# Scoring some units of a kernel-smoothing attention without the scalar engine: the difference of two clipped copies, accumulated by a second matmul with negated values, in place of an absolute value taken on VectorE

## The chip, the cores and the metric

The kernel runs on one core of a Trainium2 chip. The core has five engines with queues of their own: TensorE (PE; its weight loads are shown apart as PEld), VectorE (DVE), ScalarE (ACT), GpSimd (POOL) and SyncE (SP, which issues most DMAs). Each works off its queue in order and waits on semaphores for the others. The metric is the device time of one execution in microseconds (us). The changed kernel computes the same function.

## The reference, cut to what matters

The reference is a transformer block with two parts: an attention layer without softmax, and a mixture of 64 experts (top 8, capacity 128) with a shared expert. The inputs are 4 sequences of 2048 tokens with 256 features, in float32. The attention has 16 heads of 16 features. Every query and key is projected to one number per head, and with the bandwidth b_h of its head

```python
# out_i = sum_j max(0, 1 - |z_i - z_j|/b_h) * v_j, via prefix sums + searchsorted.
bw = jax.nn.softplus(log_bw) + BW_EPS
...
ctx = ctx / T          # T = 2048
```

where i runs over queries and j over keys. Both parts are followed by a layer norm and a residual sum:

```python
x = x + _layernorm(_L0_attn_ref(_layernorm(x), ...))
x = x + _layernorm(_L0_ffn_ref(_layernorm(x), ...))
```

The kernel does not sort. It forms the weights of all pairs of query and key directly, with q and k already divided by b_h and k negated: the score of a pair is max(0, 1 - |q + k'|) with k' = -k.

## The kernel before, in words

**The score loop.** The time is dominated by a loop of 1024 units, 256 for each of the 4 sequences. A unit is one head h, one tile s of 128 keys, and all 2048 queries. `unit(t)` (L1525) gives the order: two groups g of eight heads, in each two passes p over 4 heads, in each 16 key tiles s, and innermost the four heads j = 0 to 3. So a group is UG = 128 units long and a pass UP = 64; consecutive units have different j.

For a unit, `score(t)` (L1544) fills a tile `hat` of 128 keys by 2048 queries. Usually ACT computes |q + k'| with the key as a per-partition bias (L1558), from a tile `qb` that holds the head's queries copied to all partitions by DMA (`load_q`, L1534). Then DVE forms min(., 1) - 1 in place (L1562); this is minus the score. When a running number `spare`, an estimate of DVE's free time, is 1.3 or more, the unit goes without ACT: DVE adds the key (L1553), clears the sign bit as an integer (L1555), and does L1562 as well. This happens in 65 units; 959 go through ACT.

`product(t)` (L1579) multiplies by the values: the 128 x 32 values of a key tile are the stationary side, 512 queries of `hat` the moving side, and the result is accumulated in PSUM. The four blocks c of 512 queries are not taken from one unit: the product of step t takes block 0 of unit t, block 1 of unit t-1, block 2 of unit t-2 and block 3 of unit t-3. These units have four different j, and j sets which 32 of the 128 PSUM partitions, and so which 32 columns of PE's array, a matmul uses. In float32 a matmul shows as two records in the trace. After the last unit of a group, `evict` (L1564) copies the four accumulators out with a factor of -1/T.

Only after product(t) is the tile of unit t-3 given back. `hat`, `qb` and the evicted results `ct` are taken from one pool of 13 big tiles, first in, first out (`take`, `give`). Near the end of a pass four tiles hold the next heads' queries too.

**The background.** All other work up to the loop's end (the projections of the next sequence, and for finished sequences the layer norm, router, shared expert and experts) is cut into small tasks with an engine, an estimated cost and dependencies, and a planner (`Background`, L26) writes them into the queues between units. `step()` runs once per unit: each engine's `debt` is lowered by its `CAP` and tasks that are ready are emitted as long as the debt stays under it. So CAP is the time per unit that the planner gives an engine for background work: 0.84 us for PE, 0.65 for DVE, 0.30 for ACT; from the third sequence on PE has 0.88. Tasks that L442 names multiply by the weights of a sequence's projection (fours of matmuls of 128 x 32 by 512); those of L573 and L602 belong to the shared expert, L1041 to L1066 to the experts; L1450 and L1481 set up the first sequence's projection. `flush(tasks)` emits given tasks at once, with all that they need. The values of the next sequence are loaded tile by tile on SP as the tiles fall free (L1666); SP's queue is also that of the query loads. What is left after unit 1023 is emitted by `drain()` with other limits.

Of the kernel before, what the change touches and what calls it, by code (L numbers as in the profile page):

```python
# [8 lines left out]
F32 = mybir.dt.float32  # L9
I32 = mybir.dt.int32  # L10
AF = mybir.ActivationFunctionType
ALU = mybir.AluOpType
# [13 lines left out]
class Background:  # L26
# [3 lines left out]
           ("dve", "pe"): 1, ("dve", "sp"): 1, ("pool", "dve"): 2, ("dve", "pool"): 1, ("sp", "dve"): 4,  # L30
           ("sp", "pe"): 4, ("sp", "pool"): 4, ("sp", "act"): 5, ("sp", "sp"): 0, ("pool", "sp"): 1,
           ("act", "sp"): 1, ("pe", "sp"): 1}
    CAP = {"pe": 0.84, "dve": 0.65, "act": 0.30, "pool": 1.5, "sp": 2.0}

    def __init__(self, make):
        self.make = make
# [104 lines left out]
def sandwich_kernel(ctx: ExitStack, tc: tile.TileContext, x_in, wqT, bq, wkT, bk, wvT, bv, wprojT, log_bw,  # L141
# [84 lines left out]
    with ExitStack() as ph:  # L226
# [42 lines left out]
        def give(tag):  # L269
            bg.free["big"].append((tag, bg.t))  # L270
# [11 lines left out]
        vst = [h1[:, i * NP * VW:(i + 1) * NP * VW].rearrange("p (a w) -> p a w", a=NP) for i in range(2)]  # L282
        for t_ in vst:
            nc.gpsimd.memset(t_, 0.0)

        def slot_tile():
            tag, _ = bg.free["slot"][0]
# [1063 lines left out]

        lb = small.tile([P, H], F32, name="lb")
# [23 lines left out]
        nc.sync.dma_start(bvb, bv.rearrange("(a f) -> a f", a=1).to_broadcast([P, F]))  # L1378


        ab = small.tile([P, H], F32, name="ab")
        nc.scalar.activation(ab, lb, AF.Abs)
        ex = small.tile([P, H], F32, name="ex")
        nc.scalar.activation(ex, ab, AF.Exp, scale=-1.0)
        u = small.tile([P, H], F32, name="u")
        nc.vector.tensor_scalar_add(u, ex, 1.0)
        lu = small.tile([P, H], F32, name="lu")
        nc.scalar.activation(lu, u, AF.Ln)
        one = small.tile([P, H], F32, name="one")
        nc.vector.tensor_scalar(one, u, 1.0, None, ALU.is_equal)  # L1390
        nc.vector.tensor_add(lu, lu, one)
        den = small.tile([P, H], F32, name="den")
# [132 lines left out]
        def unit(t):  # L1525
            b, u = divmod(t, NU)
            g, w = divmod(u, UG)
            p, w = divmod(w, UP)
            s, j = divmod(w, 4)
            return b, g, p, s, j, g * GH + 2 * j + p  # L1530
# [9 lines left out]
                                  zq_d[b][m, h:h + 1, :].to_broadcast([P, HK * P]))  # L1540

        spare = [0.0]

        def score(t):  # L1544

            b, g, p, s, j, h = unit(t)
            hat[t] = take(f"hat_{b}_{h}_{s}")
            ht = hat[t][0]
            n = t // UP * 4 + j
            c = s // HK * P + h * HK + s % HK  # L1550
            k = nks[b][:, c:c + 1]
            if spare[0] >= 1.3:
                nc.vector.tensor_scalar(ht, qb[n][0], k, None, ALU.add)  # L1553
                hi = ht.bitcast(I32)
                nc.vector.tensor_scalar(hi, hi, 0x7fffffff, None, ALU.bitwise_and)  # L1555
                spare[0] -= 3.6
            else:
                nc.scalar.activation(ht, qb[n][0], AF.Abs, bias=k)  # L1558
                spare[0] += 1.9 - 1.17
            if s == NT - 1:  # L1560
                give(qb.pop(n)[1])
            nc.vector.tensor_scalar(ht, ht, 1.0, 1.0, ALU.min, ALU.subtract)  # L1562

        def evict(t):  # L1564

            for c in range(4):
                if t - 1 - c >= 0 and (t - 1 - c) % UG == UG - 1:
                    k = (t - 1 - c) // UG
                    b, g = divmod(k, NG)
                    if c == 0:  # L1570
                        ct[b, g] = take(f"ct_{b}_{g}")
                    nc.vector.tensor_scalar(ct[b, g][0][:, c * BK:(c + 1) * BK], pa.pop((k, c)), -1.0 / T, None,
                                            ALU.mult)
                    spare[0] -= 0.63
                    if c == 3 and b < B - 1:
                        nc.sync.dma_start(cx_d[b][g], ct[b, g][0])
                        give(ct.pop((b, g))[1])

        def product(t):  # L1579
            for c in range(4):  # L1580
                tt = t - c
                if not 0 <= tt < B * NU:
                    continue
                b, g, p, s, j, h = unit(tt)
                k, w = divmod(tt, UG)
                if w == 0:
                    pa[k, c] = acc.tile([P, BK], F32, tag=f"pa{c}", name=f"pa_{k}_{c}")
                nc.tensor.matmul(pa[k, c][32 * j:32 * j + 32, :],  # L1588
                                 lhsT=vt[b, s].rearrange("p a w -> p (a w)")[:, h // 2 * VW + p * D:h // 2 * VW + p * D + 32],
                                 rhs=hat[tt][0][:, c * BK:(c + 1) * BK],  # L1590
                                 start=(p == 0 and s == 0), stop=(p == 1 and s == NT - 1))
            if 3 <= t < B * NU + 3:
                give(hat.pop(t - 3)[1])

        nks, last, mst = {0: nk0}, {}, []
        scs0, chain, tabs, stored = [], [], [], [[] for b in range(B)]
# [2 lines left out]
        with tc.manual_schedule():  # L1599
            for n in range(4):  # L1600
                load_q(n)
            for t in range(B * NU + 5):
# [7 lines left out]
                if t == 0:  # L1610
# [26 lines left out]
                    last[0] = [last[0]]  # L1637
                    for i in range(1, B):
                        nks[i], last[i] = prepare(i, after=[last[i - 1]["end"]] if i > 1 else ts[-1:], mdeps=mst)
                if b == 0 and u in (28, 44):  # L1640
                    bg.flush(vts[u // 16 + 1])
                if u == 8 and b > 0:
                    finish(b - 1, after=[last[B - 1]["end"]])
                if u == 0 and b == B - 2:
                    bg.CAP = dict(bg.CAP, pe=0.88, dve=0.75, act=0.4)
                if t == B * NU - 12:
                    env = {}
                    lds = load_last(env)
# [141 lines left out]
```

## Time and profile before

| | |
|---|---|
| median of 3 runs | 2338.87 us (2335.26 to 2339.05) |
| profiled execution | 2339.91 us, span 2338.0 us |
| busy over the span | PE 84%, PEld 29%, DVE 85%, ACT 84%, POOL 21% |
| score loop, first to last min-subtract (L1562) | 66.4 to 2033.7 us |
| score activations on ACT (L1558) | 959, 1992 ns median |
| units without ACT (L1553, L1555) | 65, 1280 and 1227 ns median |
| min-subtract on DVE (L1562) | 1024, 1219 ns median |
| matmuls of the products (L1588) | 4096, two records each, 592 ns median |
| TensorE clock granted | 0.95 of full speed on average |

How to read it: the page covers one execution. Busy time counts instructions that compute. A line of a group gives the source line, engine, operation, the tiles written and read, shapes and count, then busy time and mean duration in ns, then the idle time of the engine just before, with what ended most of it ("<-PE pa" is a wait for a PE instruction on the tile pa). Records of matmuls overlap, because a matmul's end is modelled to include its way through the array; so PE's busy time overstates what PE could not have given to others. Rows of stretches give the stretch, its length, then busy time with the instruction count for PE, PEld, DVE, ACT and POOL in this order, then granted clock, DMA share and GB/s. Rows of the timeline give start, length, engine, line, operation, and the number of records merged.

### The profile page before, as it was taken

What the parts mean: (1) busy time and instruction counts of PE and PEld (TensorE: products, weight loads), DVE (VectorE), ACT (ScalarE), POOL (GpSimd) and SP (SyncE); (2) the same over time, 40 slices, a digit from 0 to 9 for tenths busy, and PEclk for the clock granted to TensorE, in tenths of its full rate; (3) what the DMA queues carried; (4) which work ended last, traced back from release to release, by engine and by line L of the source; (5) the groups of instructions that cost most, each with busy time, mean ns of one, the idle gap of its engine ahead of it and who ended that gap; (6) DMA issues with size and microseconds to landing.
All of it is one profiled execution on the core that took longest, in us unless ns stands there. A gap on an engine that the chain in (4) does not pass through costs nothing. (4 is left out here: it accounts for less than half of the span.)

```text
span 2338.0 us, 32679 instructions
## 1 busy us (share of the span) xinstructions
PE 1952.5 (84%) x12552; PEld 687.2 (29%) x12552; DVE 1996.1 (85%) x3102; ACT 1966.8 (84%) x1269; POOL 490.4 (21%) x339
## 2 busy tenths in 40 slices
PE   7898979888799899677899887878888889987783
PEld 4332323222223222112222222223332223364342
DVE  4799999898999889999989998989999979886335
ACT  2899999898999998999999998989999989742213
POOL 1001010010120000003200003446553234442463
PEclk9999999999999999989999998999999999988897
DMA  4243534427351202142302014465544243355758
GB/s 127 91 133 120 184 103 153 151 88 264 117 162 64 91 19 70 37 147 69 112 19 81 28 54 122 114 186 151 174 121 136 57 134 90 102 177 147 177 124 197
DMA packets 195078, 274.32 MB, mean 117 GB/s; under 512 B 24833, under 2 KB 165505, under 8 KB 194145
## 3 DMA queue, kind: packets, MB, share of 16 engines
q1 hardware_dynamic: 165680, 235.33, 31.2%
q0 software_dynamic: 23824, 31.70, 8.3%
q10 hardware_dynamic: 5408, 5.11, 0.7%
q8 instruction: 101, 1.65, 0.3%
q14 instruction: 65, 0.52, 0.1%
HBM read 189.18 MB, written 82.90 MB: 116 GB/s over the span
## 5 line engine op out<-in xcount | busy, mean ns | idle before, releaser
L1558 ACT ACTIVATE hat<-qb,nk 128x2048 f32<-128x2048 f32 x959 | 1837.3, 1995 | 112.8 <-DMA qb<-zq_d 57.5
L1588 PE MATMUL pa<-hat,v 128*32 128x512 f32 x8192 | 1115.3, 620 | 284.4 <-DVE hat L1562 272.3
L1562 DVE TENSOR_SCALAR hat<-hat 128x2048 f32<-128x2048 f32 x1024 | 1230.3, 1223 | 97.2 <-ACT hat L1558 91.3
L1588 PEld LDWEIGHTS pa<-hat,v 128*32 128x32 f32 x8192 | 186.2, 110 | 900.0 <-DVE hat L1562 652.6
L1066 POOL DMA_INDIRECT y_d<-s,ix x64 | 147.8, 2309 | 286.7 <-DVE s L1064 145.4
L573 PE MATMUL k<-s,sgu 128*128 128x512 f32 x352 | 198.4, 651 | 0.0
L1041 POOL DMA_INDIRECT s<-tab_d,ix x64 | 106.0, 1657 | 327.6 <-DMA qb<-zq_d 259.0
L499 POOL TENSOR_TENSOR rsc<-rsc,mhalf 128x2 f32<-128x2 f32 x24 | 53.4, 2225 | 521.2 <-DVE rsc L498 521.0
L602 PE MATMUL k<-sd,s 128*128 128x256 f32 x384 | 113.7, 428 | 16.9 <-DVE s L589 7.4
L442 PE MATMUL k<-s,s 128*32 128x512 f32 x768 | 102.4, 592 | 0.0
L602 PEld LDWEIGHTS k<-sd,s 128*128 128x128 f32 x384 | 72.2, 205 | 86.4 <-issue 47.8
L573 PEld LDWEIGHTS k<-s,sgu 128*128 128x128 f32 x352 | 54.8, 192 | 136.3 <-issue 121.2
L305 POOL TENSOR_TENSOR rsa<-rsa,mhalf 128x4 f32<-128x4 f32 x16 | 30.8, 1925 | 290.9 <-DVE rsa L304 285.6
L1553 DVE TENSOR_SCALAR hat<-qb,nk 128x2048 f32<-128x2048 f32 x65 | 83.1, 1279 | 0.1
L1555 DVE TENSOR_SCALAR hat<-hat 128x2048 int32<-128x2048 int32 x65 | 79.9, 1229 | 2.2
L350 PE MATMUL k<-h,s 128*128 128x256 f32 x256 | 73.0, 413 | 0.0
L713 DVE MAX8 codes<-scT 128x8 f32<-128x1152 f32 (+2 forms) x48 | 63.4, 1321 | 0.2
L350 PEld LDWEIGHTS k<-h,s 128*128 128x128 f32 x256 | 45.4, 195 | 54.4 <-issue 48.6
L715 DVE MATCH_REPLACE8 scT<-codes,scT 128x1152 f32<-128x1152 f32 (+2 forms) x44 | 57.6, 1310 | 0.0
L607 DVE TENSOR_SCALAR s<-k,gt 128x256 f32<-128x256 f32 x48 | 22.8, 480 | 36.5 <-PE k L602 32.0
L442 PEld LDWEIGHTS k<-s,s 128*32 128x32 f32 x768 | 31.6, 138 | 54.0 <-issue 53.2
L1258 POOL DMA_INDIRECT y_d<-v,ix x28 | 39.9, 1426 | 23.5 <-DMA y_d<-s 7.9
(319 smaller groups left out, 1643.2 us busy)
## 6 DMA issues: line engine op xcount, KB each, us to landing
qb<-zq_d SPq DMA_DIRECT2D x128, 512.0 KB, 5.5
s<-m_d SPq DMA_DIRECT2D x48, 512.0 KB, 4.8
s<-_attn_hidden_states_dram SPq DMA_DIRECT2D x28, 512.0 KB, 5.5
v_d<-h SPq DMA_DIRECT2D x48, 192.0 KB, 2.6
v<-v_d SPq DMA_DIRECT2D x48, 192.0 KB, 2.5
h<-fn_expert_gate_up_w_dram SPq DMA_DIRECT2D x32, 256.0 KB, 3.5
s<-fn_expert_gate_up_w_dram SPq DMA_DIRECT2D x32, 256.0 KB, 2.8
b<-y_d SPq DMA_DIRECT2D x16, 512.0 KB, 9.3
```

The source lines that it names most:

```text
L350: nc.tensor.matmul(env[pk][:, i * F:(i + 1) * F], lhsT=xv[:, k, o:o + P], rhs=wv[:, k, :], start=(k == 0), stop=(k == KF - 1))
L442: nc.tensor.matmul(env[pz][c * CR:(c + 1) * CR, :], lhsT=xv[:, r, :], rhs=env[mp][:, k * 2 * F:(k + 1) * 2 * F], start=(r == 0 and k == 0) ...
L573: nc.tensor.matmul(env[p_], lhsT=sgu[:, k, o:o + P], rhs=featview(env[xT])[:, k, :], start=(k == 0), stop=(k == KF - 1))
L602: nc.tensor.matmul(env[py][:, i * F:(i + 1) * F], lhsT=env[acts[f // 2]][:, o:o + P], rhs=sd[:, f, :], start=(f == 0), stop=(f == NI - 1))
L713: a = bg.add("dve", 1.25, lambda c8=c8: nc.vector.max(out=c8, in_=scT[:, :w]), ev + [a])
L1041: g = bg.add("pool", 1.3, lambda: nc.gpsimd.indirect_dma_start(out=xg(), out_offset=None, in_=tab_d[half][:, :], in_offset=bass.IndirectOf ...
L1066: s = bg.add("pool", 1.9, lambda: nc.gpsimd.indirect_dma_start(out=y_d[half][:, :], out_offset=bass.IndirectOffsetOnAxis(ap=iv(), axis=0), ...
L1553: nc.vector.tensor_scalar(ht, qb[n][0], k, None, ALU.add)
L1555: nc.vector.tensor_scalar(hi, hi, 0x7fffffff, None, ALU.bitwise_and)
L1558: nc.scalar.activation(ht, qb[n][0], AF.Abs, bias=k)
L1562: nc.vector.tensor_scalar(ht, ht, 1.0, 1.0, ALU.min, ALU.subtract)
L1588: nc.tensor.matmul(pa[k, c][32 * j:32 * j + 32, :], lhsT=vt[b, s].rearrange("p a w -> p (a w)")[:, h // 2 * VW + p * D:h // 2 * VW + p * D ...
```

## The change

Let n = -k' be the key. Two clipped copies of the queries are formed: low = q held between n-1 and n, and hat = q held between n and n+1. For q above n, low is n and hat - low is min(q - n, 1); for q below n, hat is n and hat - low is min(n - q, 1). So hat - low = min(|q + k'|, 1), and minus the score is hat - low - 1. A clipped unit therefore makes two tiles, `low` and `hat`, with one DVE instruction each, reading two per-partition operands (columns of n-1, n, n+1), and accumulates both: `hat` with the values and `low` with the negated values. The missing -1 times the sum of the values of all clipped units is taken off when a group is evicted.

In detail:

- In `score`, a unit with `spare` of 1.3 or more takes the clipped form if it lies between units 4 and 115 of its group and if the pool has at least 3 to 5 free big tiles; otherwise it takes the old form. It takes a second big tile, forms the three columns (a DVE operation on 128x3), negates the 128x32 values (DVE), adds the values to a running sum per head (POOL), and clips twice (DVE). `spare` is lowered by 2.7 (3.6 for the old form), and PE's debt is raised by 1.1.
- In `product`, each of the four blocks of a clipped unit gets a second matmul ahead of its own, with the same destination. The low tile is given back together with the hat tile.
- At unit 120 of each group `sums` multiplies the sums with a column of ones (four small matmuls) and DVE copies the result to `csum`; this is flushed in place. POOL clears the sums at the start of a group.
- `evict` subtracts `csum` (a per-partition operand) before the factor -1/T.
- PE's CAP goes from 0.84 to 0.86, and from the third sequence on from 0.88 to 0.92.
- A new small tile `pro` holds the sums, the columns and two buffers of negated values, and before the loop the temporaries of the bandwidth, which had tiles of their own.

In the order of instructions that results, 62 units are clipped, 17 take the old form and 945 go through ACT.

```diff
-    CAP = {"pe": 0.84, "dve": 0.65, "act": 0.30, "pool": 1.5, "sp": 2.0}
+    CAP = {"pe": .86, "dve": 0.65, "act": 0.30, "pool": 1.5, "sp": 2.0}
...
+        pro = small.tile([P, 12 * D + 8], F32, name="pro")
+        near = const.tile([P, 3], F32, name="near")
+        csum = const.tile([P, 1], F32, name="csum")
+        for i in range(3):
+            nc.gpsimd.memset(near[:, i:i + 1], i - 1.0)
...
+        def value(t):
+
+            b, g, p, s, j, h = unit(t)
+            o = h // 2 * VW + p * D
+            return vt[b, s].rearrange("p a w -> p (a w)")[:, o:o + 2 * D]
+
+        def sums():
+
+            env = {}
+
+            def mm():
+                for j in range(4):
+                    nc.tensor.matmul(env["cs"][2 * D * j:2 * D * j + 2 * D, :1], lhsT=pro[:, 2 * D * j:2 * D * j + 2 * D],
+                                     rhs=near[:, 2:3], start=True, stop=True)
+            q, bg.q = bg.q, []
+            a = bg.add("pe", 0.4, mm, get={"cs": "bank"}, env=env)
+            a = bg.add("dve", 0.15, lambda: nc.vector.tensor_copy(csum, env["cs"][:, :1]), [a], put=["cs"], env=env)
+            bg.q += q
+            bg.flush([a])
...
-            if spare[0] >= 1.3:
-                nc.vector.tensor_scalar(ht, qb[n][0], k, None, ALU.add)
-                hi = ht.bitcast(I32)
-                nc.vector.tensor_scalar(hi, hi, 0x7fffffff, None, ALU.bitwise_and)
-                spare[0] -= 3.6
+            u = t % NU
+            if u % UG == 0:
+                nc.gpsimd.memset(pro[:, :8 * D], 0.0)
+            room = 3 + (s >= 9) + (u % UG >= UG - 24)
+            if spare[0] >= 1.3 and 4 <= u % UG < UG - 12 and len(bg.free["big"]) >= room and (True):
+
+                low[t] = take(f"low_{b}_{h}_{s}")
+                i = len(clipped) % 2
+                kk = pro[:, 12 * D + 4 * i:12 * D + 4 * i + 3]
+                neg[t] = pro[:, (8 + 2 * i) * D:(10 + 2 * i) * D]
+                tot = pro[:, 2 * D * j:2 * D * j + 2 * D]
+                nc.vector.tensor_scalar(kk, near, k, None, ALU.subtract)
+                nc.vector.tensor_scalar(neg[t], value(t), -1.0, None, ALU.mult)
+                nc.gpsimd.tensor_tensor(out=tot, in0=tot, in1=value(t), op=ALU.add)
+                nc.vector.tensor_scalar(low[t][0], qb[n][0], kk[:, 0:1], kk[:, 1:2], ALU.max, ALU.min)
+                nc.vector.tensor_scalar(ht, qb[n][0], kk[:, 1:2], kk[:, 2:3], ALU.max, ALU.min)
+                clipped.add(t)
+                spare[0] -= 2.7
+                bg.debt["pe"] += 1.1
             else:
-                nc.scalar.activation(ht, qb[n][0], AF.Abs, bias=k)
-                spare[0] += 1.9 - 1.17
+                if spare[0] >= 1.3:
...
+                    spare[0] -= 3.6
+                else:
+                    nc.scalar.activation(ht, qb[n][0], AF.Abs, bias=k)
+                    spare[0] += 1.9 - 1.17
+                nc.vector.tensor_scalar(ht, ht, 1.0, 1.0, ALU.min, ALU.subtract)
...
-                    nc.vector.tensor_scalar(ct[b, g][0][:, c * BK:(c + 1) * BK], pa.pop((k, c)), -1.0 / T, None,
-                                            ALU.mult)
+                    nc.vector.tensor_scalar(ct[b, g][0][:, c * BK:(c + 1) * BK], pa.pop((k, c)), csum, -1.0 / T,
+                                            ALU.subtract, ALU.mult)
...
+                if tt in low:
+                    nc.tensor.matmul(pa[k, c][32 * j:32 * j + 32, :], lhsT=neg[tt], rhs=low[tt][0][:, c * BK:(c + 1) * BK],
+                                     start=False, stop=False)
...
+                if u % UG == UG - 8:
+                    sums()
...
-                    bg.CAP = dict(bg.CAP, pe=0.88, dve=0.75, act=0.4)
+                    bg.CAP = dict(bg.CAP, pe=.92, dve=0.75, act=0.4)
```

More of the change, by code (lines that the diff above doesn't have):

```diff
@@ L1350, in norm_x0 @@
             xt0.append(done)
-        lb = small.tile([P, H], F32, name="lb")
+        lb, ab, ex, u, lu, one, den = (pro[:, i * H:(i + 1) * H] for i in range(7))
         nc.sync.dma_start(lb, log_bw.rearrange("(a h) -> a h", a=1).to_broadcast([P, H]))
@@ L1378, in sandwich_kernel @@
         nc.sync.dma_start(bvb, bv.rearrange("(a f) -> a f", a=1).to_broadcast([P, F]))
-        ab = small.tile([P, H], F32, name="ab")
         nc.scalar.activation(ab, lb, AF.Abs)
-        ex = small.tile([P, H], F32, name="ex")
         nc.scalar.activation(ex, ab, AF.Exp, scale=-1.0)
-        u = small.tile([P, H], F32, name="u")
         nc.vector.tensor_scalar_add(u, ex, 1.0)
-        lu = small.tile([P, H], F32, name="lu")
         nc.scalar.activation(lu, u, AF.Ln)
-        one = small.tile([P, H], F32, name="one")
         nc.vector.tensor_scalar(one, u, 1.0, None, ALU.is_equal)
         nc.vector.tensor_add(lu, lu, one)
-        den = small.tile([P, H], F32, name="den")
         nc.vector.tensor_scalar_sub(den, u, 1.0)
@@ L1542, in sandwich_kernel @@
         spare = [0.0]
+        low, neg, clipped = {}, {}, set()
+        def value(t):
[13 more added lines that the diff above has]
+            bg.flush([a])
         def score(t):
@@ L1551, in score @@
             k = nks[b][:, c:c + 1]
-            if spare[0] >= 1.3:
-                nc.vector.tensor_scalar(ht, qb[n][0], k, None, ALU.add)
-                hi = ht.bitcast(I32)
-                nc.vector.tensor_scalar(hi, hi, 0x7fffffff, None, ALU.bitwise_and)
-                spare[0] -= 3.6
-            else:
-                nc.scalar.activation(ht, qb[n][0], AF.Abs, bias=k)
-                spare[0] += 1.9 - 1.17
+            u = t % NU
[16 more added lines that the diff above has]
+                bg.debt["pe"] += 1.1
+            else:
+                if spare[0] >= 1.3:
+                    nc.vector.tensor_scalar(ht, qb[n][0], k, None, ALU.add)
+                    hi = ht.bitcast(I32)
+                    nc.vector.tensor_scalar(hi, hi, 0x7fffffff, None, ALU.bitwise_and)
+                    spare[0] -= 3.6
[3 more added lines that the diff above has]
+                nc.vector.tensor_scalar(ht, ht, 1.0, 1.0, ALU.min, ALU.subtract)
             if s == NT - 1:
                 give(qb.pop(n)[1])
-            nc.vector.tensor_scalar(ht, ht, 1.0, 1.0, ALU.min, ALU.subtract)
         def evict(t):
@@ L1587, in product @@
                     pa[k, c] = acc.tile([P, BK], F32, tag=f"pa{c}", name=f"pa_{k}_{c}")
[L1588 to L1591, printed above, removed]
+                first_, last_ = p == 0 and s == 0, p == 1 and s == NT - 1
+                if tt in low:
+                    nc.tensor.matmul(pa[k, c][32 * j:32 * j + 32, :], lhsT=neg[tt], rhs=low[tt][0][:, c * BK:(c + 1) * BK],
+                                     start=False, stop=False)
+                nc.tensor.matmul(pa[k, c][32 * j:32 * j + 32, :], lhsT=value(tt), rhs=hat[tt][0][:, c * BK:(c + 1) * BK],
+                                 start=first_, stop=last_)
             if 3 <= t < B * NU + 3:
                 give(hat.pop(t - 3)[1])
+                if t - 3 in low:
+                    give(low.pop(t - 3)[1])
         nks, last, mst = {0: nk0}, {}, []
```

## The prediction

> **What bounds the kernel now.** I read first the busy shares, then the score loop alone (64 to 2034 us, units 0 to 1023), then its groups by line and shape, then who waited, then short timelines. The profiled execution took 2339.9 us, a span of 2338.0 and 1.9 around it; the median of the runs is 2338.9, so 1.0 is taken off at the end.
>
> ```profile
> 64.00:2034.00 1970.00, 1684.59 (x11323) 525.11 (x11327) 1798.16 (x2415) 1871.45 (x1082) 356.49 (x195) 0.97 0.36 110
> ```
>
> This row (length, then busy PE, PEld, DVE, ACT, POOL, then clock and DMA) covers 84% of the time. ACT is busy 95% of it, DVE 91%, PE 86%. Three engines are near full, so the bound changes from stretch to stretch. The groups give the prices:
>
> ```profile
> L1558 ACT ACTIVATE hat<-qb,nk 128x2048 f32<-128x2048 f32 x959 | 1837.3, 1995 | 112.8 <-DMA qb<-zq_d 57.5 <-PE pa L1588 49.6 <-DMA cx_d<-ct 3.1
> L1588 PE MATMUL pa<-hat,v 128*32 128x512 f32 x8192 | 1115.3, 620 | 284.4 <-DVE hat L1562 272.3
> ```
>
> ```profile
> L1562 DVE TENSOR_SCALAR hat<-hat 128x2048 f32<-128x2048 f32 x1024 | 1230.3, 1223 | 97.2 <-ACT hat L1558 91.3
> L1553 DVE TENSOR_SCALAR hat<-qb,nk 128x2048 f32<-128x2048 f32 x65 | 83.1, 1279 | 0.1
> L1555 DVE TENSOR_SCALAR hat<-hat 128x2048 int32<-128x2048 int32 x65 | 79.9, 1229 | 2.2
> L309 DVE TENSOR_SCALAR s<-s,mva,rsa 128x256 f32<-128x256 f32 x64 | 23.4, 412 | 2.3 <-POOL rsa L305 2.3
> L607 DVE TENSOR_SCALAR s<-k,gt 128x256 f32<-128x256 f32 x48 | 22.8, 480 | 36.5 <-PE k L602 32.0
> ```
>
> An ACT unit costs ACT 1837.3/959 = 1.916 us and DVE 1.20; one of the 65 units without ACT costs DVE 1.28 + 1.23 + 1.20 = 3.71. PE's price needs the timeline, where the count is of half-matmuls (each matmul shows as two records):
>
> ```profile
> 71.31 1.05 PE L1588 MATMUL pa<-hat,v 128*32 128x512 f32 x4
> 74.45 1.06 PE L1588 MATMUL pa<-hat,v 128*32 128x512 f32 x6 [1.03 <-DVE hat L1562]
> 76.58 1.06 PE L1588 MATMUL pa<-hat,v 128*32 128x512 f32 x8
> ...
> 391.57 1.92 PE L1588 MATMUL pa<-hat,v 128*32 128x512 f32 x16
> ...
> 393.58 3.90 ACT L1558 ACTIVATE hat<-qb,nk 128x2048 f32<-128x2048 f32 x2 [0.27 <-PE pa L1588]
> ```
>
> Two, three or four matmuls of one product take the same 1.05 us: they go to different 32-column groups of the array and run side by side. Two products back to back take 1.92, so a further turn of the same column groups costs 1.92 - 1.06 = 0.86. The last line shows ACT itself held by PE, through a tile that PE had not released. That happens where background matmuls are dense. Units 16-47, 96-127, 176-191 and 272-287, same columns as above:
>
> ```profile
> 101.40:156.20 54.80, 54.80 (x524) 23.04 (x524) 52.22 (x52) 52.52 (x29) 0.00 (x0) 1.00 0.25 87
> 244.90:299.30 54.40, 54.40 (x504) 18.54 (x504) 50.94 (x47) 49.06 (x27) 0.00 (x0) 1.00 0.59 181
> 389.30:418.30 29.00, 29.00 (x266) 9.84 (x268) 24.93 (x26) 25.33 (x14) 0.00 (x0) 1.00 0.59 190
> 574.20:598.30 24.10, 24.10 (x228) 8.01 (x224) 23.34 (x21) 23.43 (x13) 0.00 (x0) 1.00 0.58 175
> ```
>
> In these 162 us PE is never idle, while ACT has 12.0 us left and DVE 10.9.
>
> **The change, part by part.** Counts are from the changed kernel's instruction order.
>
> ACT: 945 score activations in place of 959. Only 14 go, because 62 clipped units and 17 of the old form replace 65: at most 14 x 1.916 = -26.8 us. Where they go matters more; see below.
>
> DVE: the old form loses 65 - 17 = 48 pairs, 48 x 2.51 = -120.5; the min-subtract loses 62, 62 x 1.20 = -74.5. Each clipped unit adds two clips with two per-partition operands and two small operations. A clip appears nowhere. L309 has two such operands and two operations on 256 elements: 412 ns. L607, whose source is PSUM, has one operand and takes 480. So L309 passes elements faster than L607; if L1562's 2048 elements in 1223 ns and L309 share a rate, and two operands add twice the 56 ns by which L1553 exceeds L1562, a clip is 1223 + 112 = 1335 ns. The other end is L607's rate: twice the streaming, about 2.4 us. I take 1.34, as L309 is the nearest row in form. The small ones I put at 0.2 each (128x4 operations take 168 to 216 ns). A clipped unit is 2 x 1.34 + 0.4 = 3.08, and 62 are +191. Evictions gain a pointer operand, 32 x 0.06 = +2. DVE sum: -2 us, nothing.
>
> PE: 248 further matmuls of 128x32 by 512. Each goes to the same column group as the one behind it in its product, since both accumulate into the same 32 partitions. It can't run beside it. So each costs 0.86, a clipped unit 3.44 over its four products, 213 us in all; the floor is the average of a packed matmul, 1115.3/4096 = 0.27, or 67 us. I take 0.86. The planner is told 1.1 per clipped unit, so it moves only 68 us of background aside.
>
> By the Trainium skill (TensorE: Matmul & The Clock Gate, Part 3, What overlaps and what doesn't) matmuls start and end strictly in program order, which would put the other three matmuls of a product behind the pair as well. By that rule nothing of the 213 us could be hidden inside a product; by the trace's packed average it would be 67. No row of before shows two matmuls of one product on one column group.
>
> Where that falls: the background matmuls that fill PE now lie at units 10-57 (L1450, L1481), 104-139, 188-231 and 280-317 (L442), against 10-50, 96-128, 176-208 and 256-288 before. In these zones are 7, 3, 9 and 4 clipped units. What PE needs there, against the time that the same units took before (starts of their L1562):
>
> - 188-231: 44 products x 0.86 + 32 background fours x 0.86 + 9 x 3.44 = 37.8 + 27.5 + 31.0 = 96 us; before 85. +11.
> - 280-317: 32.7 + 27.5 + 13.8 = 74; before 69. +5.
> - 104-139: 31.0 + 27.5 + 10.3 = 69; before 65. +4.
> - 10-57: 41.3 + 36 (before's rate there, 1.71 a unit less 0.86, over 41 units, and 1 for the rest) + 24.1 = 101; before 85. +16.
>
> And in units 400-447 (the shared expert's matmuls) PE had 3.4 us idle of 91; five clipped units add 17.2, of which the planner moves 5.5 aside: +8.
>
> Sum +44. The tiles let PE fall behind: a tile comes back to ACT 4.8 units after its release (counted in the order), some 9 us, of which one unit's way through ACT, DVE and PE needs 1.9 + 1.2 + 1.1, so about 5 are margin. A stretch may end that much late and make it up in the emptier units behind; I take 3 for each of the five: +29. The other 34 clipped units lie where PE has 10 to 40% idle; I cost them at nothing, the cover being that idle time. Without cover each costs up to 3.44 - 1.1 = 2.34, 80 us.
>
> The ACT saving, zone by zone: inside the four zones the units without ACT go from 16 to 29, so 13 of the 14 lie where PE sets the pace, and outside it is one: -2 us.
>
> New waits: eight times a loop a group's value sum is flushed in place. DVE's copy of it stands behind four small matmuls and the product before them, about 1.06 + 0.66 (four small transposes at L1047 show 0.66), then 0.2: 15 us in which DVE's queue, and behind it the next min-subtracts, stand. DVE's 172 idle us cover it at one end, 15 at the other; I take +5. POOL gets 62 adds of 128x32 (its 128x2 to 128x256 rows are 0.2 to 2.2 us); nobody waits but that flush, 12 units later, and 17 of the 48 value loads on SP, which now also wait for POOL, with query loads queued behind them: 0.
>
> The end: two more of the experts' turns and four more shared matmuls lie after the loop, in 304 us that hold 68 turns; the matmuls are four of 1.1 us: between 0 and 13, +2 as PE is 75% busy there.
>
> Sum: 29 - 2 (ACT) + 5 + 2 - 2 (DVE) = **+32**: 2339.9 + 32 - 1.0 = **2371 us**.
>
> **The rivals.**
>
> *PE hides it (faster).* In zone 188-231 the clipped units cost nothing as long as one takes PE under (85 - 65.3)/9 = 2.2 us, 0.55 per matmul. For it: column groups are served side by side, so those without the pair can run ahead, and by total PE has 285 idle us for 213. Against it: the background is of full width and needs all groups. Then ACT's -26.8 stands, with the +7 of flushes and end: 2319.
>
> *Tiles run short (no change).* One of 13 big tiles is held for four units more. From a tile's release to its next score the order gives 5.2 units on average before, 4.8 after; four units: 95 cases to 266, three or less: 68 to 97. In the trace ACT's wait before a score grows from 0.07 us at five units to 0.37 at four and 0.51 at three. Weighted with where in a phase they lie, that is +24, which cancels ACT's gain even if PE hides its part: 2337.
>
> *Clips at half the rate (slower still).* 124 x 1.07 = +133 us on DVE, against 172 idle; in the zones it adds to PE's loss: about +75, 2414. L309 speaks against it.
>
> *POOL holds SP.* At the change to the last batch POOL is in its gathers, where one wait for DVE was 14.4 us; a value load behind it holds the query loads: +14 on the main case, 2385.
>
> **How the numbers follow.** PE's column cost 0.48, PE hides it 0.33, no change 0.10, half-rate clips 0.05, POOL 0.04. The likeliest gives 2371, on its own 2354 (the five stretches use their whole 5 us of margin, flushes and end cost nothing) to 2394 (ten clipped units more uncovered). The range, 2314 to 2405, takes in the faster case and leaves out the half-rate clips and the tails. 0.2% (4.7 us) is about what a measurement tells from no change: faster 0.33, same 0.10, slower 0.57.
>
> **What would show it.** Score activations 945; clips near 1.34 us (2.4 would be the half rate). A product with a clipped unit about 1.9 us long, not 1.06. PE busy in the loop near 1850 us and fully busy over units 188-231, and those 44 units some 8 us longer; ACT's waits for PE well over 49.6. If a product of ten records takes under 1.6 us, or the zones run no longer than before, the main step is wrong.

## The result, and the profile after

The changed kernel takes **2470.09 us** (median; 2466.93 to 2476.59), against 2338.96 us (2335.26 to 2342.61) for the kernel before: a ratio of 1.0564, 95% interval 1.0536 to 1.0593. It is slower by 131 us, where the forecast said 32 slower, and lies above the range. The profiled execution has a span of 2466.2 us, 128.2 more than before.

Of these 128.2 us, 119 lie in the score loop (first score to last, 1970.6 us before and 2089.7 after), 11 after it (303.2 and 314.6), and 2 are gained ahead of it. Busy times of the page after:

```profile
PE 2131.2 (86%) x13112; PEld 754.8 (31%) x13112; DVE 1988.5 (81%) x3200; ACT 1947.4 (79%) x1253; POOL 523.4 (21%) x412
```

PE is busy 179 us more (1952.5 before), which is only 2% more of the longer span (84% before), and DVE and ACT fell from 85 and 84% to 81 and 79: by these shares no engine became the bound. The same row for the loop alone (length, then busy PE, PEld, DVE, ACT, POOL, clock, DMA):

```profile
63.90:2150.40 2086.50, 1857.13 (x11861) 591.29 (x11861) 1788.21 (x2508) 1851.20 (x1064) 381.51 (x258) 0.98 0.34 103
```

PE's 1857 us are near the 1850 that the prediction named, and 172.5 more than before: 0.70 for each of the 248 matmuls, where its price of 0.86 gives 213. So PE got no more work than was foreseen; what the work does to the time was not foreseen. The groups of after (busy us, mean ns, idle time before them and who ended it):

```profile
L1600 ACT ACTIVATE hat<-qb,nk 128x2048 f32<-128x2048 f32 x945 | 1818.1, 1995 | 242.5 <-PE pa L1634 144.9 <-DMA qb<-zq_d 59.1 <-PE pa L1632 13.5
L1634 PE MATMUL pa<-hat,v 128*32 128x512 f32 x8192 | 1307.5, 614 | 223.5 <-DVE hat L1602 213.4 <-DVE ct L1614 3.8 <-DVE hat L1589 2.5
L1602 DVE TENSOR_SCALAR hat<-hat 128x2048 f32<-128x2048 f32 x962 | 1161.0, 1223 | 151.3 <-ACT hat L1600 148.0
L1588 DVE TENSOR_SCALAR low<-qb,pro 128x2048 f32<-128x2048 f32 x62 | 84.3, 1360 | 9.2 <-PE pa L1634 7.3 <-PE pa L1632 1.3
L1589 DVE TENSOR_SCALAR hat<-qb,pro 128x2048 f32<-128x2048 f32 x62 | 83.2, 1341 | 0.0
```

The clips cost what was expected. But ACT now stands 144.9 us behind PE's products (49.6 before), and DVE stands 148.0 behind ACT (91.3 before). The products' own group grew by 192 us in busy time (1115.3 before) although it has no instruction more: a matmul that has to wait for the one on its column group spreads its product out. Here is one such product (start, length, records of half-matmuls), with the background matmul behind it:

```profile
435.64 0.62 PE L1634 MATMUL pa<-hat,v 128*32 128x512 f32 x1
435.65 0.62 PE L1632 MATMUL pa<-low,pro 128*32 128x512 f32 x1
435.66 1.03 PE L1634 MATMUL pa<-hat,v 128*32 128x512 f32 x3
436.10 0.59 PE L1632 MATMUL pa<-low,pro 128*32 128x512 f32 x1
436.12 1.44 PE L1634 MATMUL pa<-hat,v 128*32 128x512 f32 x4
437.48 1.13 PE L357 MATMUL k<-h,s 128*128 128x256 f32 x4
```

From the product's start to the background matmul's it is 1.84 us; a product without a pair takes 1.07 (median of those standing alone) and one with a pair 1.92 (median of all 248). The rule of the Trainium skill that the prediction weighed (TensorE: Matmul & The Clock Gate, Part 3, What overlaps and what doesn't: matmuls start and end in program order) fits this in size. The order itself is not shown by this row: the two records of `low` start 0.45 us apart, with three of `hat` between them. So that the background matmul waits behind the pair is seen; whether the product's other matmuls do stays open.

Where in the loop the time went, by the starts of the min-subtracts (the second clip for a clipped unit):

| units | before, us | after, us | difference | predicted |
|---|---|---|---|---|
| 10-57 | 85.3 | 99.6 | +14.4 | +16 |
| 104-139 | 65.2 | 74.0 | +8.8 | +4 |
| 188-231 | 85.2 | 93.9 | +8.7 | +11 |
| 280-317 | 68.9 | 77.7 | +8.8 | +5 |
| 400-447 | 91.3 | 101.7 | +10.4 | +8 |
| the five, with lag made up | | | +51 | +44 - 15 |
| 448-511 | 117.2 | 129.5 | +12.3 | 0 |
| 704-767 | 121.0 | 136.9 | +15.9 | 0 |
| 960-1022 | 122.3 | 138.7 | +16.4 | 0 |
| all else | | | +23 | 0 |

The five stretches that were called full lost 51 us, and the units behind each of them took longer too: 58-103 by 6.7 us, 140-187 by 3.7, 232-279 by 5.0, 318-399 by 0.3. In 188-231 PE is busy all the time, as foreseen:

```profile
439.80:533.70 93.90, 93.90 (x681) 34.01 (x679) 69.95 (x75) 67.74 (x36) 5.30 (x7) 1.00 0.37 118
```

The rest of the loop, costed at about nothing, lost 68. The stretch 704-767 before and then after shows why this is not seen in busy shares:

```profile
1408.60:1529.60 121.00, 96.15 (x656) 30.36 (x648) 105.30 (x116) 108.65 (x67) 52.31 (x25) 0.93 0.46 123
```

```profile
1492.20:1629.10 136.90, 111.87 (x703) 33.79 (x699) 105.48 (x136) 109.08 (x66) 49.01 (x27) 0.96 0.38 104
```

PE was 79% busy there. It got 15.7 us more to do, had 24.9 us idle, and the stretch became longer by 15.9: the added work came on top, and the idle time stayed (25.0 us after).

### The profile page after: what moved, and what is told of

Same layout as the page of the kernel before. It is cut to its first block, busy times and chain, and to the rows that moved or that the text cites. A ratio compares the mean times of both kernels' runs of the same rounds, so it can differ in the third digit from the quotient of the medians.

```text
span 2466.2 us, 33990 instructions
## 1 busy us (share of the span) xinstructions
PE 2131.2 (86%) x13112; PEld 754.8 (31%) x13112; DVE 1988.5 (81%) x3200; ACT 1947.4 (79%) x1253; POOL 523.4 (21%) x412
## 5 line engine op out<-in xcount | busy, mean ns | idle before, releaser
L1600 ACT ACTIVATE hat<-qb,nk 128x2048 f32<-128x2048 f32 x945 | 1818.1, 1995 | 242.5 <-PE pa L1634 144.9
L1634 PE MATMUL pa<-hat,v 128*32 128x512 f32 x8192 | 1307.5, 614 | 223.5 <-DVE hat L1602 213.4
L1602 DVE TENSOR_SCALAR hat<-hat 128x2048 f32<-128x2048 f32 x962 | 1161.0, 1223 | 151.3 <-ACT hat L1600 148.0
L1634 PEld LDWEIGHTS pa<-hat,v 128*32 128x32 f32 x8192 | 240.0, 109 | 892.0 <-DVE hat L1602 534.1
L1632 PE MATMUL pa<-low,pro 128*32 128x512 f32 x496 | 258.4, 603 | 4.3 <-DVE low L1588 4.1
L449 PE MATMUL k<-s,s 128*32 128x512 f32 x768 | 164.1, 598 | 0.0
L609 PE MATMUL k<-sd,s 128*128 128x256 f32 x352 | 101.7, 418 | 9.4 <-DVE s L614 9.4
L1588 DVE TENSOR_SCALAR low<-qb,pro 128x2048 f32<-128x2048 f32 x62 | 84.3, 1360 | 9.2 <-PE pa L1634 7.3
L1589 DVE TENSOR_SCALAR hat<-qb,pro 128x2048 f32<-128x2048 f32 x62 | 83.2, 1341 | 0.0
L449 PEld LDWEIGHTS k<-s,s 128*32 128x32 f32 x768 | 50.0, 140 | 50.8 <-issue 49.0
L1632 PEld LDWEIGHTS pa<-low,pro 128*32 128x32 f32 x496 | 42.8, 109 | 71.3 <-issue 49.0
```

Of the source, the lines that this page charges most:

```text
L449: nc.tensor.matmul(env[pz][c * CR:(c + 1) * CR, :], lhsT=xv[:, r, :], rhs=env[mp][:, k * 2 * F:(k + 1) * 2 * F], start=(r == 0 and k == 0) ...
L609: nc.tensor.matmul(env[py][:, i * F:(i + 1) * F], lhsT=env[acts[f // 2]][:, o:o + P], rhs=sd[:, f, :], start=(f == 0), stop=(f == NI - 1))
L1588: nc.vector.tensor_scalar(low[t][0], qb[n][0], kk[:, 0:1], kk[:, 1:2], ALU.max, ALU.min)
L1589: nc.vector.tensor_scalar(ht, qb[n][0], kk[:, 1:2], kk[:, 2:3], ALU.max, ALU.min)
L1632: nc.tensor.matmul(pa[k, c][32 * j:32 * j + 32, :], lhsT=neg[tt], rhs=low[tt][0][:, c * BK:(c + 1) * BK], start=False, stop=False)
L1634: nc.tensor.matmul(pa[k, c][32 * j:32 * j + 32, :], lhsT=value(tt), rhs=hat[tt][0][:, c * BK:(c + 1) * BK], start=first_, stop=last_)
```

## The experiments

Four theories stood after the result. *Column theory*: the second matmul on a column group is what costs, and PE's idle time takes none of it. *Tile theory*: the second tile held for four units. *Placement theory*: the planner's new limits and the units' places. And the *flush* of the sums. In the table, loop and end (after the last score) are from the profiled executions; where a kernel leaves out a part of the computation, the work after the loop still has the changed kernel's number of matmuls and of indirect transfers unless it is said otherwise. Each ratio is to the kernel before in the same round of runs. Its median was 2333.8 to 2339.0 us over the rounds, so a difference between medians of two rounds is good to some 5 us.

| run | ratio to before, 95% interval | median us | loop us | end us | PE busy us |
|---|---|---|---|---|---|
| before | 1 | 2338.96 | 1970.6 | 303.2 | 1952.5 |
| after | 1.0564 (1.0536-1.0593) | 2470.09 | 2089.7 | 314.6 | 2131.2 |
| a1_one_column | 1.0128 (1.0108-1.0148) | 2366.35 | 1993.3 | 308.3 | 1972.0 |
| a2_no_tile | 1.0519 (1.0499-1.0540) | 2458.24 | 2082.3 | 306.9 | 2115.4 |
| a6_no_tile_one_column | 1.0023 (1.0007-1.0038) | 2339.10 | 1961.9 | 314.8 | 1960.0 |
| a4_old_only | 1.0116 (1.0096-1.0136) | 2362.91 | 1977.7 | 319.6 | 1950.5 |
| e1_pairs | 1.0550 (1.0519-1.0582) | 2463.98 | 2099.9 | 303.2 | 2119.4 |
| e2_packed | 1.0131 (1.0089-1.0173) | 2363.39 | 2001.7 | 307.0 | 1998.6 |
| e3_tile_held | 1.0078 (1.0051-1.0105) | 2354.86 | 1990.0 | 300.7 | 1956.5 |
| a3_no_flush | 1.2834 (1.2799-1.2870) | 2999.53 | 2070.3 | 859.9 | 2323.5 |
| e4_outside | 1.0343 (1.0317-1.0369) | 2413.70 | 2045.3 | 301.5 | 2056.1 |
| e6_spread | 1.0307 (1.0273-1.0340) | 2405.32 | 2046.1 | 300.6 | 2108.3 |
| b1_limits | 1.0105 (1.0085-1.0125) | 2359.84 | 1975.4 | 318.6 | 1950.1 |
| g1_two_units | 1.0354 (1.0334-1.0374) | 2417.73 | 2040.4 | 312.8 | 2055.9 |
| c1_limits_back | 1.0507 (1.0476-1.0537) | 2450.74 | 2084.8 | 300.7 | 2125.2 |
| c3_two_units_limits_back | 1.0544 (1.0515-1.0573) | 2461.38 | 2068.5 | 327.3 | 2061.9 |
| c2_lower | 1.0014 (0.9996-1.0032) | 2340.55 | 1972.3 | 303.8 | 1955.0 |

### One column in place of 512 (a1_one_column)

```diff
-nc.tensor.matmul(pa[k, c][32 * j:32 * j + 32, :], lhsT=neg[tt], rhs=low[tt][0][:, c * BK:(c + 1) * BK],
+nc.tensor.matmul(pa[k, c][32 * j:32 * j + 32, :1], lhsT=neg[tt], rhs=low[tt][0][:, c * BK:c * BK + 1],
```

> The changed kernel with its 248 extra products cut from 512 columns to one: low*(-v) is left out but for one column in 512. The clips, the second tile, the order and the planner's numbers stay. Column theory (the 0.85 us that a product with a pair takes beyond one without is time that nothing hides, 213 us of PE in all): PE loses about 200 us of busy time, a product with a pair falls from 1.92 to about 1.1 us, and most of the +131 goes: 2340 to 2375 us. Tile theory (62 units hold two of the 13 big tiles, so the writers run out of tiles): the tiles are held as long as before, so 2440 to 2470. Placement theory (the planner's limits and the units taken off ScalarE in the wrong stretches): 2430 to 2470.

Measured 2366.35 us: 104 of the 131 are gone with nothing changed but the width of 248 matmuls. Of the loop 96.4 us go, for 159 us of PE. A product whose pair is one column wide, again with the background matmul behind it:

```profile
413.76 0.62 PE L1634 MATMUL pa<-hat,v 128*32 128x512 f32 x2
413.78 0.19 PE L1632 MATMUL pa<-low,pro 128*32 128x1 f32 x1
413.79 0.62 PE L1634 MATMUL pa<-hat,v 128*32 128x512 f32 x1
413.83 0.17 PE L1632 MATMUL pa<-low,pro 128*32 128x1 f32 x1
413.86 1.02 PE L1634 MATMUL pa<-hat,v 128*32 128x512 f32 x5
414.82 1.13 PE L357 MATMUL k<-h,s 128*128 128x256 f32 x4
```

It is 1.06 us to the next matmul in place of 1.84 (at the median 1.05, against 1.00 behind a product without a second matmul). So the columns streamed a second time through a column group are the cost, not the instruction.

### No second tile, alone and with one column (a2_no_tile, a6_no_tile_one_column)

```diff
-                low[t] = take(f"low_{b}_{h}_{s}")
+                low[t] = hat[t]
...
-                    give(low.pop(t - 3)[1])
+                    low.pop(t - 3)
```

> The changed kernel without a second tile: the first clip is written to the unit's own tile, the second clip overwrites it, and both matmuls of the pair read that tile, so low is lost. Instructions and their counts stay. Column theory: as the changed kernel, 2440 to 2470, with products of a pair at 1.9 us. Tile theory: most of the +131 goes, 2350 to 2390. Both in parts: in between; then the shares of this run and of the run with one column are to be added and set against the run with both.

> Both edits at once: no second tile, and the extra products one column wide (low's part of the computation is left out). If columns and tiles are all that the change costs: 2335 to 2360 us. If the placement of the units, the planner's limits or the sums cost as well, it stays above 2380. If the effects of the two edits add up, the saving is the sum of those of the two single edits; if either alone frees the same wait, it is that of the larger one.

Alone, the missing tile saves 12 us (7.4 of the loop). Together with the narrow matmuls it saves 27 more than these alone do (31.4 of the loop), and the kernel is back at 2339 us. So the tile is a second, smaller cost, and it shows fully only where PE doesn't already set the pace. With both gone the loop is 8.7 us shorter than before, flush and limits included, where the 14 activations fewer are 26.8 us of ACT's busy time. It is 24 us shorter in the five stretches, where all of these 14 lay (20 units without ACT before, 34 after), and 16 longer elsewhere, where 18 us of the flush fall.

### The old form alone, and the limits alone (a4_old_only, b1_limits)

The first is the changed kernel with no unit clipped, the second the kernel before with two numbers changed:

```diff
-            if spare[0] >= 1.3 and 4 <= u % UG < UG - 12 and len(bg.free["big"]) >= room and (True):
+            if spare[0] >= 1.3 and 4 <= u % UG < UG - 12 and len(bg.free["big"]) >= room and (False):
```

```diff
-    CAP = {"pe": 0.84, "dve": 0.65, "act": 0.30, "pool": 1.5, "sp": 2.0}
+    CAP = {"pe": .86, "dve": 0.65, "act": 0.30, "pool": 1.5, "sp": 2.0}
...
-                    bg.CAP = dict(bg.CAP, pe=0.88, dve=0.75, act=0.4)
+                    bg.CAP = dict(bg.CAP, pe=.92, dve=0.75, act=0.4)
```

> The changed kernel with no clipped unit at all: units not done by ScalarE take the old form (add, then mask), csum stays zero and its flush is left out; the planner's limits .86 and .92, the new order of small tiles and the longer eviction stay. Placement theory in so far as it is the planner's limits: slower than before by 20 us or more. Column and tile theories: within 10 us of before, 2330 to 2349.

> The kernel before with the changed kernel's planner limits for PE (.86 for .84 and .92 for .88) and nothing else. If the limits alone make the end after the score loop longer (it took 320 us in the changed kernel without clipped units, against 303): 2350 to 2365, with an end of 315 to 320 us. If not: within 5 us of before, and the 16 us come from elsewhere in the changed code.

The old form alone is 27 us slower than before, which neither column nor tile theory allows; the limits alone cost 26 (15.4 in the end, 4.8 in the loop, by the profiles; the profiled execution of before lies 6 us above the median of that round). So the limits explain it, and the other small edits (small tiles, the pointer operand of the eviction) nothing that can be seen. The stretch after the loop, before and then with the new limits:

```profile
2034.90:2338.00 303.10, 218.79 (x855) 131.85 (x852) 168.69 (x586) 81.54 (x164) 124.65 (x110) 0.85 0.66 160
```

```profile
2039.50:2358.10 318.60, 221.20 (x863) 132.76 (x863) 169.95 (x588) 81.61 (x165) 129.25 (x112) 0.84 0.63 153
```

PE has 2.4 us more to do there and POOL 4.6, and the end is 15.5 longer. So the amount of work left over doesn't account for it. Its order may; that was not traced.

### Pairs, packed matmuls and held tiles in the kernel before (e1_pairs, e2_packed, e3_tile_held)

```diff
+                if tt in old:
+                    nc.tensor.matmul(pa[k, c][32 * j:32 * j + 32, :], lhsT=zw, rhs=hat[tt][0][:, c * BK:(c + 1) * BK],
+                                     start=False, stop=False)
```

```diff
+            for c in range(4):
+                if t - 3 in old:
+                    k, j = (t - c) // UG, (t - c) % 4
+                    nc.tensor.matmul(pa[k, c][32 * j:32 * j + 32, :], lhsT=zw, rhs=hat[t - c][0][:, c * BK:(c + 1) * BK],
+                                     start=False, stop=False)
```

```diff
+                if len(bg.free["big"]) >= 3 + (s >= 9) + (t % UG >= UG - 24):
+                    idle[t] = bg.free["big"].pop(0)[0]
...
+                    if t - 3 in idle:
+                        give(idle.pop(t - 3))
```

`old` holds the units of the old form, `zw` zero weights. The first stands ahead of a block's own matmul, the second after the four of a product.

> The kernel before with 224 further matmuls with zero weights, one in each of the four products of the 56 units in the old form that lie where the changed kernel allows a pair; each goes to the same column group as its own matmul. The result is unchanged, no tile, clip or unit is added. Column theory: products with such a pair take 1.9 us in place of 1.07, PE gains 224 x 0.86 = 193 us of busy time, and the kernel is slower by 70 to 120 us, 2410 to 2460. Tile theory and placement theory: within 20 us of before, as PE's slack takes it.

> The kernel before with the same number of matmuls with zero weights as in the run of pairs, but the four of a unit's step lie in four different column groups, as a further product of four. Column theory: 56 further turns of about 0.86 to 1.07 us, 48 to 60 us of PE, and the kernel is slower by 10 to 40 us; a quarter to a third of what the pairs cost. If the number of matmuls or of their columns counts, and not the column group: the same as the pairs.

> The kernel before with an unused big tile taken out of the pool at each unit in the old form, by the changed kernel's rule for room, and given back with the unit's own tile four units later. No instruction is added. Tile theory: slower by 40 us or more, with ScalarE waiting longer on PE at the units after. Column theory and placement theory: within 10 us of before.

224 pairs bring the kernel before to 2464 us, nearly the changed kernel's time, with none of its clips, tiles, sums or limits; the end is untouched. As many matmuls on four different column groups cost 25 us in place of 126. So it is the further turn that is paid. A further turn costs PE 0.75 us as a pair (166.9/224) and 0.82 as a packed four (46.1/56), close to the 0.86 of the prediction. The held tiles cost 17 us, between the two theories' values; the pairs cost a little more than the column theory's range.

### Pairs where PE has idle time, and pairs spread out (e4_outside, e6_spread)

```diff
-                if 4 <= t % UG < UG - 12:
+                if 4 <= t % UG < UG - 12 and not (10 <= t <= 57 or 104 <= t <= 139 or 188 <= t <= 231 or 280 <= t <= 317 or 400 <= t <= 447):
                     old.add(t)
```

```diff
-                if tt in old:
+                if tt % 4 == 0 and 4 <= tt % UG < UG - 12 and c == tt // 4 % 4:
```

> The kernel before with the pairs of zero-weight matmuls at the 38 old-form units alone that lie outside the five stretches which the prediction counted as full (10-57, 104-139, 188-231, 280-317, 400-447): 152 further matmuls. Cost at nothing there, as the prediction had it (PE has 10 to 40% idle at them): within 10 us of before. If PE's idle time can't take them: the 72 us that the run with all 56 units lost outside the five stretches, so 2400 to 2420, 1.9 us for each unit.

> The kernel before with 224 zero-weight matmuls again, but one in every fourth unit (one of its four products) in place of four in each of 56 units: the same work for PE in small pieces. If the cost is PE's time on average: as the run of pairs, 2440 to 2480. If it is the burst, four products running in which PE falls 3.4 us behind while the 13 tiles hold only some units of work: much less, 2350 to 2400.

The first tests the very step that cost nothing in the prediction. Its 38 units lie outside the five stretches, and the loop is 74.7 us longer (the median 80): 2.0 us for each unit, 0.72 us for each us that PE got to do. PE's idle time hid a quarter. (11 of the 74.7 us fall inside the five stretches, where no pair stands; outside them it is 64, 1.7 for each unit.) Why it hides so little is seen at unit 749. Before (start, length, engine, instruction, idle before it):

```profile
1503.52 1.23 DVE L1562 TENSOR_SCALAR hat<-hat 128x2048 f32<-128x2048 f32 x1
1505.51 0.48 DVE L1064 TENSOR_SCALAR s<-k,s 128x256 f32<-128x256 f32 x1 [0.76 <-PE k L1061]
1505.91 1.22 DVE L1562 TENSOR_SCALAR hat<-hat 128x2048 f32<-128x2048 f32 x1
```

and with the pair of that unit:

```profile
1547.78 1.23 DVE L1567 TENSOR_SCALAR hat<-hat 128x2048 f32<-128x2048 f32 x1
1552.32 0.48 DVE L1064 TENSOR_SCALAR s<-k,s 128x256 f32<-128x256 f32 x1 [3.32 <-PE k L1061]
1552.72 1.22 DVE L1567 TENSOR_SCALAR hat<-hat 128x2048 f32<-128x2048 f32 x1
```

The middle instruction belongs to an expert of the background and takes a result of PE (k). PE's matmul for it comes 2.5 us later here, behind the four widened products; and DVE takes its queue in order, so the next min-subtract stands behind that. It isn't a tile that is late here, and no stock of tiles helps. The waits of DVE for such results over the whole execution, before and with these pairs (total us, times, longest):

```profile
DVE s L607 <- PE k L602: 32.0, 22, 3.6
...
DVE s L1054 <- PE k L1047: 12.0, 16, 2.2
DVE s L1064 <- PE k L1061: 11.0, 13, 2.7
```

```profile
DVE s L607 <- PE k L602: 39.1, 25, 3.8
DVE s L1064 <- PE k L1061: 30.5, 26, 4.6
DVE s L1054 <- PE k L1047: 21.4, 19, 2.8
```

Summed over the loop, DVE's waits for PE ahead of such instructions are 69 us before, 123 here, 130 after (16.6 of them for csum), and 86 in the changed kernel with one column (14.7 for csum). ACT's waits for tiles rose too: 49.6 us before, 144.9 after, and here

```profile
ACT hat L1563 <- PE pa L1596: 99.2, 84, 5.7
```

That is 50 us more, as much as DVE's 54. No run took one of the two away and left the other, so the share of each stays open.

The same matmuls one at a time, in every fourth unit, give PE nearly as much (155.8 us) and cost the loop 75.5 us in place of 129. The time, 2405 us, lies between the two expectations. A single further turn (0.70 us) is hidden by half, four in a row by a quarter. The runs differ in place as well: of the 224 turns 50 lie in the five stretches here, 72 in the run of pairs. Outside the stretches a spread turn costs 0.25 us (43.7/174), one of four in a row 0.42 (63.7/152, from the run of 38 units). That the spread ones lie mostly at units done by ACT, and the pairs at units of the old form, was not tested apart.

### Without the flush (a3_no_flush)

```diff
-                if u % UG == UG - 8:
-                    sums()
```

> The changed kernel without the sums of the values and their flush, eight times (csum stays zero, so the correction by the sum of the values is left out). If the flush costs what its idle time before DVE says (16.6 us over eight): 2450 to 2462. If it is taken up by the waits beside it: 2465 to 2475. If it empties the pipeline each time (more than 5 us each): below 2430.

The total misled: 2999.53 us. Without the correction the context is another, and with it what the router decides: after the loop there are 182 indirect transfers in place of 53, in 859.9 us in place of 314.6 (in the loop 117 and 118). Only the loop can be compared: 2070.3 us, 19.4 shorter than after, and 17.8 of this lie around the flushes, from unit 116 of each group to unit 11 of the next. So the eight flushes cost about 2.4 us each, near the 16.6 us for which DVE stands before them:

```profile
DVE csum L1562 <- PE k L1558: 16.6, 8, 3.8
```

### Two units in a row, and the limits back (g1_two_units, c1_limits_back, c3_two_units_limits_back, c2_lower)

```diff
-            if spare[0] >= 1.3 and 4 <= u % UG < UG - 12 and len(bg.free["big"]) >= room and (True):
+            second = t - 1 in clipped and t - 2 not in clipped
+            if (second or spare[0] >= 1.3 and 4 <= u % UG < UG - 12 and len(bg.free["big"]) >= room + 1) and len(bg.free["big"]) >= 2:
...
         def product(t):
             for c in range(4):
                 tt = t - c
+                if tt in low:
+                    k, j = tt // UG, tt % 4
+                    nc.tensor.matmul(pa[k, c][32 * j:32 * j + 32, :], lhsT=neg[tt], rhs=low[tt][0][:, c * BK:(c + 1) * BK],
+                                     start=False, stop=False)
+            for c in range(4):
+                tt = t - c
...
-                if tt in low:
-                    nc.tensor.matmul(pa[k, c][32 * j:32 * j + 32, :], lhsT=neg[tt], rhs=low[tt][0][:, c * BK:(c + 1) * BK],
-                                     start=False, stop=False)
```

These are the edits of the first run. The second sets the two limits of the changed kernel back to .84 and .88, the third does both, and the last sets those of the kernel before to .82 and .86.

> The changed kernel with the clipped units taken two in a row (28 times two, 56 in all, for 62 single ones), and the extra matmuls of a product set ahead of its four ordinary ones, so that two units need five further turns for eight extra matmuls (140 in all for 248). The result is unchanged. Column theory with shared turns: PE loses about 80 us of busy time, and the kernel gains 30 to 50 us on the changed one, 2420 to 2440. If each extra matmul costs its own time: 2455 or more. Tile theory: slower than the changed kernel, as four tiles are held for two units at once.

> The changed kernel with the planner's limits for PE of before (.84 and .88), all else as changed. If the 26 us that the limits cost in the kernel before are a part of the changed kernel's loss: 2440 to 2450, with an end near 303 us after the loop. If the clipped units use up what the limits give: 2460 to 2475, or slower still, as the background work of PE is pushed later.

> The changed kernel with clipped units two in a row and shared further turns, and with the planner's limits of before. If the two savings add up (52 and 26): 2385 to 2400. If not: 2405 to 2420. Faster than before only if the PE turns left (140 of 0.72 us, by the run of pairs some 60 us of time) were hidden by something else, which no theory here says: not expected.

> The kernel before with lower planner limits for PE (.82 for .84, .86 for .88). If the time falls with the limit as it rose with it (26 us for the step up): 2310 to 2320, faster than both kernels. If the limits of before stand at the best point, or the effect is the chance of where two or three background jobs fall: 2333 to 2360.

Shared turns work: 108 turns fewer take 75 us off PE and 52 off the time. With the limits back the changed kernel gains 19 us (16 when each is set against the kernel before of its own round). Its end is 300.7 us, 14 shorter; the plan also clips 58 units in place of 62, so the loop's 5 us are not the limits' alone. The two edits together were expected at 2385 to 2400 and gave 2461: 28 us more in the loop than with two units in a row alone, and an end of 327.3 us. There more background was left after the loop (925 matmul records against 868), in a plan that clips 52 units. Why this plan is worse in the loop was not found; it shows that effects of the planner's numbers don't add. Lower limits in the kernel before change nothing that can be told. No version here beats the kernel before; that with neither pair nor tile, which leaves out a part of the computation, only equals it.

## Why the prediction was wrong

The direction was right, the size was not: 131 us against 32. Step by step:

- **PE's price (0.86 for each further matmul, 213 us): right as a length, too high as busy time.** Products with a pair take 1.92 us, 0.85 more than without. PE's busy time in the loop rose by 172.5 us to 1857, 0.70 for each. (The 1850 that the prediction named isn't what its terms give: 1685 and 213 make 1898.) With narrow matmuls 96 of the loop's 119 us go, and pairs alone make the kernel before as slow.
- **"The other 34 clipped units lie where PE has 10 to 40% idle; I cost them at nothing": the step that failed.** Outside the five stretches the loop lost 68 us. 39 of them go with the narrow matmuls (51 between the two kernels without the second tile), 1.2 to 1.5 us for each of the 34 units; the flush is 18 more. In the kernel before, pairs at such places alone cost 1.7 to 2.0 us for each unit. So half and more of the text's own price without cover, up to 2.34 each, was paid. The idle time was poor cover: before, 272 of PE's 284 idle us ahead of products ended with DVE's min-subtract, so PE was idle because the chain ACT, DVE, PE hadn't reached it, and a lag put into the chain moves all of it.
- **"I take 3 for each of the five" (lag made up later): failed as well.** The stretches were priced at +44 and lost 51, and the units behind them took longer too. The run with pairs at all 56 units differs from that with 38 by the pairs inside the stretches alone; it is 46 us longer there and 8 longer outside, so nothing was made up. The margin was counted in tiles. DVE and ACT also take PE's background results in queue order, and the tiles give no margin for that.
- **The end, +2: mis-sized, measured 11,** inside the text's own bound of 13. The planner's limits were in the diff and got no term of their own. Alone they cost 26 us; in the changed kernel, taking them back gains 16 to 19, of which 14 are the end.
- **The flush, +5: mis-sized, 19** by the loop without it; the end of the bound that the text gave, 15, was nearer.
- **Clips, 1.34 us; small operations, 0.2: right.** The clips have a median of 1347 and 1342 ns, the small ones 222 and 173. ACT's gain of 2 was not measured apart; that the gain is lost where PE sets the pace fits the 24 us by which the five stretches are shorter when pair and tile are gone.

Of the rivals, *PE hides it* and *half-rate clips* are out by these numbers. *POOL holds SP* is not seen: ACT's waits for query loads are 57.5 us before and 59.1 after. *Tiles run short* was a real cost but a second one: 7 us of the loop beside the pairs, 31 without them, 17 us of the time with held tiles alone. By single undoings the terms are 96 (pairs) + 7 (tile) + 19 (flush) + 11 (end) - 2 (start) = 131, against the 128.2 of the spans; that this closes so well is partly luck, since the first two overlap.

## What to carry to other kernels

An idle share of an engine is cover only if the engine can work ahead in it. Ask what ends its idle time: if it is the previous stage of the same chain, added work moves the whole chain, here by 0.5 to 0.8 us for each us, and less in the run with small pieces than in those with bursts. When queues are worked off in order, look for every instruction that takes the delayed engine's result, background jobs included, before a lag is said to be taken up by buffers. And a changed number in a planner is a change of its own: it needs its own term, or its own run.

## What the runs showed of the hardware

- A product with two matmuls on one column group takes 1.92 us, 1.07 without the second; with the second at one column in place of 512 the background matmul behind starts 1.05 us after the product, in place of 1.00 without a second. Eight extra matmuls of two neighbouring units, set ahead of a product's own, share turns: 0.70 us of PE for each turn saved (75.3/108).
- Clips of 128x2048 float32 with two per-partition operands take 1342 to 1347 ns at the median, against 1219 before for min and subtract with two constants.
